# Five chunks of six of a normalized token block turned by VectorE squares and a trip through memory, and its columns kept in triples

## The chip, the cores and the metric

The kernel runs on one NeuronCore of one Trainium2 chip. The metric is the device time of one execution in microseconds (us). Three runs of the kernel before took 1774.83, 1776.05 and 1778.08 us; the median, 1776.05 us, is the time before.

## What is computed

The input `x` holds 8 images of 128 channels and 48 x 48 = 2304 positions (tokens), all in float32. Two layers follow each other; cut to what matters here:

```
# layer 0: causal attention over the tokens, queries and keys from a group-normed x and position rows
x = x + conv_attention(group_norm(x))            # softmax over the lower triangle, 128 channels
# layer 1, on tokens t = x seen as (image, token, channel)
xh = (t - mean(t)) / sqrt(var(t) + 1e-5)         # over the 128 channels of a token
t  = t + softmax(xh @ xh.T) @ xh                 # full self-attention of the 2304 tokens
t2 = layer_norm(t)
t  = t + scan(sigmoid, batch_norm(t2 @ W.T), V)  # a recurrence over the tokens
```

The change concerns `xh`. The product `xh @ xh.T` contracts over channels, so TensorE needs `xh` with the channels on the 128 partitions (channel-major). The product of the softmax with `xh` contracts over tokens, so it needs `xh` with the tokens on the partitions (token-major). The kernel holds both forms of an image.

## The kernel before, in words

An image is cut into 6 chunks of 384 tokens (`QC`), a chunk into 3 blocks of 128 (`QB`). `fast_path` walks over the images. For each one a `Causal` part goes through layer 0's attention and a `Full` part through layer 1's attention; the list `stream` (line 1414) is the order of all their items. One item is a score matmul (`begin`), an exponential on ScalarE, and three items later (`LAG`) the matmul with the values (`product`). A float32 matmul stands in the trace as two instructions.

After the last item of causal chunk j, `Causal.after` (line 1042) adds a chain of steps that makes chunk j of `xh`. For chunks 0 to 4 (`far`) it is: `store` (VectorE has turned the result in 32 x 32 squares at line 953; SyncE writes it to memory, line 961), `turn` (line 1062: VectorE transposes the softmax sums into the single-buffered tile `ta` and reduces them), `load` (line 967: four transfers bring the result back token-major), `sums` (TensorE adds the sums up, line 1072, and VectorE takes reciprocals), `residual` (line 1086, and the moments at lines 915 and 916), `rooted` (GpSimd, line 924), `normed` (line 929: VectorE writes the token-major chunk `c["y"]`, a part of `xhT`), and `back` (line 1103: three transposes on TensorE at line 934 into the PSUM tile `tb`, and one ScalarE copy at line 1105 into the channel-major tile `xh`). Chunk 5 takes the same steps, except that its result gets token-major by TensorE (`oc_t`) and not through memory.

The order of the work is written out by a planner, `Stream` (lines 548 to 601). It keeps a planned time `now` that TensorE work moves on (`spend`), and a planned time `at` from which a chain's next step may be put out. `tick`, after each item, puts out up to two steps that are due, in the order in which the chains were added. What it decides is only the order of the instructions in each engine's queue; at run time every queue is worked off in that order, and each instruction waits for its operands. `chunk_tile` (line 689) with a holder forces an earlier chain on to a given step before its tile is taken again.

`Full.begin` (line 1191) asks in chunk j = 0 that chunk n of `xh` has been put out before item 3n (line 1196), then issues the score matmul (line 1214), whose two operands are a block of 128 columns and a chunk of 384 columns of `xh`. The other half of the symmetric scores is not computed again: `turned` (line 1177) transposes the exponentials in squares, `store` (line 1157) writes them to memory as `e`, and `load` (line 1148) brings them back as `g`. All these transfers are issued by SyncE, whose queue is worked off in order; so are the position rows `pb` (line 845), the tokens `t1t` (line 1060), and `t_d` and `t2x` of the second normalization.

A recurrence of 36 steps for three segments follows at the end (line 1547).

Of the kernel before, what the change touches and what calls it, by code (L numbers as in the profile page):

```python
# [14 lines left out]
F32 = mybir.dt.float32  # L15
# [589 lines left out]
def fast_path(ctx: ExitStack, tc: tile.TileContext, x, pe, w_ffn, out, x_tok, w_qkv, w_pos, v_t, gamma_beta, flag):  # L605
    nc = tc.nc
    B, C, H, W = x.shape
    N = H * W
    P = 128
# [3 lines left out]
    QC = 384  # L613
    NQ = N // QC
    QB = QC // P
# [6 lines left out]
    dpool = ctx.enter_context(tc.tile_pool(name="dram", bufs=1, space=DRAM))  # L622
# [17 lines left out]
    SQ = 32  # L640
    R = P // SQ
# [22 lines left out]
    with ExitStack() as actx:  # L664
# [19 lines left out]
        def psum_t(name):  # L684
            return ps_t.tile([P, CH], F32, tag="t", name=name)
# [3 lines left out]
        def chunk_tile(tag, name, holder=None, steps=0, bufs=2):  # L689

            if holder is not None:
                before = holders.setdefault(tag, deque([({}, 0)] * bufs))
                old, n = before.popleft()
                before.append((holder, steps))
                if "chain" in old:
                    st.advance(old["chain"], n)
            return (work if bufs == 2 else work1).tile([P, QC], F32, tag=tag, name=name)
# [247 lines left out]
        def turn_result(o, name, holder, blocks_first):  # L945

            ot = chunk_tile("o", f"ot_{name}", holder, 1)
            dst, src = ot.rearrange("p (a g c) -> p a g c", a=R, g=QB), o[:, :QC]
            if blocks_first:
                dst, src = dst.rearrange("p a g c -> p g a c"), src.rearrange("p (g a r) -> p g a r", a=R, g=QB)  # L950
            else:
                src = src.rearrange("p (a g r) -> p a g r", a=R, g=QB)
            nc.vector.transpose(dst, src)
            return ot
# [16 lines left out]
        def block_of(to, g):  # L971

            return to.rearrange("p (k g c) -> p g k c", g=QB, c=SQ)[:, g]

        def by_block(tile_ap):

            return tile_ap.rearrange("p (g a r) -> p a g r", a=R, g=QB)
# [3 lines left out]

        t1_tok, x_hat, normed_chunks = {}, {}, {}

        class Causal:


# [55 lines left out]
            def after(self, j, o):  # L1042
                b = self.b
                cols = ts(j, QC)
                acc = self.sums.pop(j)[1]
                c = self.whose.pop(j)

                far = CAUSAL_FAR and j < NQ - 1
                if far:
                    ot = turn_result(o, f"c_{b}_{j}", c, False)  # L1050
                    at = st.then(st.now, [("DVE", 0.57)])
                    through = token_major(c, ot, f"c_{b}_{j}", "toc", 5)
                else:
                    o_sb = chunk_tile("o", f"oc_{b}_{j}", c, 3)
                    nc.scalar.copy(by_block(o_sb), o[:, :QC].rearrange("p (a g r) -> p a g r", a=R, g=QB))
                    at = st.then(st.now, [("ACT", 0.5)])
                    through = []

                y = t1p.tile([P, QC], F32, tag="t1t", name=f"t1t_{b}_{j}")
                nc.sync.dma_start(y, x_tok[b, j])  # L1060

                def turn():
                    ta = chunk_tile("ta", f"ta_{b}_{j}", bufs=1)
                    nc.vector.transpose(ta, acc)
                    c["parts"] = small.tile([P, R * QB], F32, tag="parts", name=f"parts_{b}_{j}")
                    nc.vector.tensor_reduce(c["parts"], ta.rearrange("p (k c) -> p k c", c=SQ), AX.X, ALU.add)

                def sums():

                    tp = psum_t(f"dn_{b}_{j}")  # L1070
                    k = R * QB
                    nc.tensor.matmul(tp[:, :k], same.rearrange("p a c -> p (a c)"), c["parts"], start=True, stop=True)  # L1072
                    own = small.tile([P, R, QB], F32, tag="ownc", name=f"ownc_{b}_{j}")
                    nc.vector.tensor_mul(own.rearrange("p a g -> p (a g)"), tp[:, :k], mine[:, 0].rearrange("p a g -> p (a g)"))
                    ri = small.tile([P, QB], F32, tag="ric", name=f"ric_{b}_{j}")
                    nc.vector.tensor_reduce(ri, own.rearrange("p a g -> p g a"), AX.X, ALU.add)
                    nc.vector.reciprocal(ri, ri)
                    c["ri"] = ri

                def residual():  # L1080
                    to = None if far else transposed(o_sb, f"oc_t_{b}_{j}")
                    for g in range(QB):
                        yg = y[:, ts(g, P)]
                        if far:
                            yg = yg.rearrange("p (k c) -> p k c", k=R)
                        nc.vector.scalar_tensor_tensor(
                            yg, block_of(c["o"], g) if far else to[:, ts(g, P)], c["ri"][:, g : g + 1], yg, ALU.mult, ALU.add
                        )
                    t1_tok[b, j] = y
                    c["mv"], c["ve"] = moments(y, f"c{b}_{j}", "l1")  # L1090

                def rooted():
                    c["rs"] = root(c["ve"], f"c{b}_{j}", "l1")

                def normed():
                    if j == 0:
                        x_hat[b] = (
                            big.tile([P, NB, P], F32, tag="xhT", name=f"xhT_{b}"), big.tile([P, N], F32, tag="xh", name=f"xh_{b}")
                        )
                    c["y"] = x_hat[b][0][:, QB * j : QB * (j + 1), :].rearrange("p g c -> p (g c)")  # L1100
                    normalize(c["y"], t1_tok[b, j], c["mv"], c["rs"])

                def back():
                    tp = transposed(c["y"], f"tb_{b}_{j}")
                    nc.scalar.copy(x_hat[b][1][:, cols], tp[:, :QC])

                c["chain"] = normed_chunks[b, j] = st.add([
                    *through[:1],
                    (turn, 0.0, [("DVE", 1.05)]),
                    *through[1:],  # L1110
                    (sums, 0.15, [("DVE", 0.55)]),
                    (residual, 0.0 if far else 0.35, [("DVE", 2.6)]),
                    (rooted, 0.0, [("POOL", 0.9)]),
                    (normed, 0.0, [("DVE", 1.1)]),
                    (back, 0.35, [("ACT", 0.5)]),
                ], max(at, st.free["DVE"]) + 0.2 - st.now)

        class Full:
# [72 lines left out]
            def begin(self, j, what, first):  # L1191
                b = self.b
                if first and j == 0:
                    self.rows = small2.tile([P, NB, NQ], F32, tag="rows", name=f"rows_{b}")
                if j == 0:
                    st.finish(normed_chunks[b, what[1] // QB])
                if first and b + 1 < B:
                    if j == 1:
                        norm_chain[b + 1] = st.add(group_norm(b + 1))
                    if j == NQ - 2:  # L1200
                        st.finish(norm_chain[b + 1])
                        project(b + 1, 0)
                self.prefetch()
                if what[0] == "turned":
                    i, g = what[1:]
                    while (i, j) not in self.loaded:
                        while self.pairs[len(self.loaded)] not in self.stored:
                            self.store()
                        self.load()
                    return self.loaded[i, j][:, :, g, :, :].rearrange("p a m r -> p m a r"), 0.0  # L1210
                m = what[1]
                xh = x_hat[b][1]
                s = psum_s(f"s1_{b}_{j}_{m}")
                nc.tensor.matmul(s[:, :QC], xh[:, ts(m, P)], xh[:, ts(j, QC)], start=True, stop=True)  # L1214
                p = pp.tile([P, QC], F32, tag="p", name=f"p1_{b}_{j}_{m}")
                nc.scalar.activation(p, s[:, :QC], AF.Exp, bias=shift, accum_out=self.rows[:, m, j : j + 1])  # L1216
                return p, st.then(st.spend(QC * US), [("ACT", 0.58)])
# [208 lines left out]
        for n in range(len(stream) + LAG):  # L1426
            if n < len(stream):
                part, j, what, first, last = stream[n]
                ready[n] = part.begin(j, what, first)
            if n >= LAG:  # L1430
                part, j, what, first, last = stream[n - LAG]
# [16 lines left out]
    with ExitStack() as rctx:  # L1448
# [32 lines left out]
        a = rc.tile([P, 1], F32, tag="bn_a", name="bn_a")  # L1481
        rsqrt(rc, a, mv[:, 1:2], 1e-5, "bn")
        nc.vector.tensor_mul(a, a, gb[:, 0:1])
        c = rc.tile([P, 1], F32, tag="bn_c", name="bn_c")
# [19 lines left out]
        prev, warm, y = [], [], [None] * G  # L1504
# [7 lines left out]
        d = rc.tile([P, G, B, SG], F32, tag="d", name="d")  # L1512
# [25 lines left out]
        for t in range(-WARM, LS):  # L1538
            s = t % TZ
# [93 lines left out]
```

## Time and profile before

| What | Value |
|---|---|
| Median of three runs | 1776.05 us |
| Span of the profiled execution (first to last instruction) | 1772.5 us |
| What lies around the span, against the median | 3.55 us |
| Mean granted TensorE clock | 0.993 |
| TensorE busy | 1742.7 us (98%) |
| VectorE busy | 1302.8 us (74%) |
| ScalarE busy | 764.8 us (43%) |
| GpSimd busy | 195.2 us (11%) |
| Transposes `tb`, line 934 | 144 of 273 ns, 23.6 us busy |
| Copies `xh<-tb`, line 1105 | 48 of 478 ns |
| Score matmuls `s<-xh`, line 1214 | 504 in 1008 instructions, 410.4 us busy |
| SyncE transfers | 257.47 MB |

The page gives no own time of the profiled execution apart from its span; the three runs were timed without the profiler. In the profile, PE is TensorE's matmuls, PEld its weight loads, DVE VectorE, ACT ScalarE, POOL GpSimd and SP SyncE; a q behind the name is the engine's queue, with its transfers and waits. A group of instructions is told by line, engine and operation, then what it writes and reads. Busy times of TensorE overlap where matmuls are pipelined; the chain of work that ended last gives each piece the time by which it moved the end. Images repeat: the main loop has a period of 207.7 us per image, and the views below look at the third image (about 463 to 671 us).

### The profile page before, as it was taken

What the parts mean: (1) busy time and instruction counts of PE and PEld (TensorE: products, weight loads), DVE (VectorE), ACT (ScalarE), POOL (GpSimd) and SP (SyncE); (2) the same over time, 40 slices, a digit from 0 to 9 for tenths busy, and PEclk for the clock granted to TensorE, in tenths of its full rate; (3) what the DMA queues carried; (4) which work ended last, traced back from release to release, by engine and by line L of the source; (5) the groups of instructions that cost most, each with busy time, mean ns of one, the idle gap of its engine ahead of it and who ended that gap; (6) DMA issues with size and microseconds to landing.
All of it is one profiled execution on the core that took longest, in us unless ns stands there. A gap on an engine that the chain in (4) does not pass through costs nothing.

```text
span 1772.5 us, 22223 instructions
## 1 busy us (share of the span) xinstructions
PE 1742.7 (98%) x6231; PEld 1093.2 (62%) x6231; DVE 1302.8 (74%) x3363; ACT 764.8 (43%) x1842; POOL 195.2 (11%) x303
## 2 busy tenths in 40 slices
PE   8999999999999999999999999999999999999996
PEld 5666566665666566665666656665666656665565
DVE  4868668876887668786687767876687866877467
ACT  2344434443345434444344433454344543444455
POOL 1110011100110001100111001100011001110006
PEclk8999999999999999999999999999999999999998
DMA  4405672257533584156732575335941468116768
GB/s 140 138 23 187 182 204 94 87 184 188 145 103 128 159 226 141 34 176 182 200 99 80 188 192 152 106 111 161 237 129 50 160 183 214 45 65 198 194 211 216
DMA packets 206056, 262.00 MB, mean 148 GB/s; under 512 B 90113, under 2 KB 175010, under 8 KB 205412
## 3 DMA queue, kind: packets, MB, share of 16 engines
q1 hardware_dynamic: 204972, 257.47, 49.4%
q0 software_dynamic: 720, 2.62, 1.0%
q8 instruction: 52, 0.85, 0.2%
q14 instruction: 80, 0.66, 0.1%
q10 hardware_dynamic: 232, 0.40, 0.1%
HBM read 150.24 MB, written 110.17 MB: 147 GB/s over the span
## 4 chain that ended last, share of the span: by engine, by line
PE 96%; DMA 1%; DVE 1%; ACT 0%; issue 0%; SPq 0%; POOL 0%; ACTq 0%; POOLq 0%; DVEq 0%
PE o L1228 18%; PE s L1214 18%; PE s L1013 17%; PE o L1024 17%; PE o L1224 13%; PE pj L874 4%; PE pj L877 2%; PE z L1547 2%; PE wx L1320 2%; PE of_t L934 1%; PE tb L934 1%; PE pb L832 0%; DMA x<-in_x_dram 0%; PE dn L1072 0%; PE ts L1259 0%
## 5 line engine op out<-in xcount | busy, mean ns | idle before, releaser
L1216 ACT ACTIVATE p<-s,shift 128x384 f32<-128x384 f32 x504 | 292.4, 580 | 479.7 <-PE s L1214 464.2
L1015 ACT ACTIVATE p<-s 128x384 f32<-128x384 f32 (+2 forms) x504 | 231.8, 460 | 424.8 <-PE s L1013 377.5
L1214 PE MATMUL s<-xh 128*128 128x384 f32 x1008 | 410.4, 489 | 0.0
L1228 PE MATMUL o<-p,xhT 128*128 128x384 f32 x1008 | 404.1, 488 | 5.9 <-ACT p L1216 5.9
L1013 PE MATMUL s<-q,k 128*128 128x384 f32 (+2 forms) x1008 | 381.5, 460 | 0.2 <-DVE k L884 0.2
L1024 PE MATMUL o<-p,vT 128*128 128x384 f32 (+2 forms) x1008 | 377.4, 456 | 0.0
L1224 PE MATMUL o<-g,xhT 128*128 128x384 f32 x720 | 281.3, 488 | 1.1 <-DMA g<-e 1.1
L1228 PEld LDWEIGHTS o<-p,xhT 128*128 128x128 f32 x1008 | 188.9, 190 | 133.8 <-ACT p L1216 10.5
L1024 PEld LDWEIGHTS o<-p,vT 128*128 128x128 f32 x1008 | 188.8, 190 | 114.7 <-issue 0.6
L1214 PEld LDWEIGHTS s<-xh 128*128 128x128 f32 x1008 | 186.2, 190 | 115.3
L1013 PEld LDWEIGHTS s<-q,k 128*128 128x128 f32 x1008 | 182.6, 191 | 97.3 <-issue 1.0
L1039 DVE TENSOR_TENSOR acc<-acc,p 128x384 f32<-128x384 f32 (+2 forms) x408 | 208.8, 512 | 33.4 <-POOL p L1018 8.7
L1177 DVE STREAM_TRANSPOSE t<-p 128x384 f32<-128x384 f32 x360 | 187.3, 550 | 37.6 <-ACT p L1216 32.8
L1224 PEld LDWEIGHTS o<-g,xhT 128*128 128x128 f32 x720 | 133.2, 190 | 83.7 <-DMA g<-e 1.3
L1185 DVE TENSOR_REDUCE tsum<-t 128x12 f32<-128x1152 f32 x120 | 162.3, 1353 | 4.2
L879 DVE TENSOR_TENSOR z<-pj,pb 128x384 f32<-128x384 f32 x144 | 78.8, 547 | 108.8 <-PE pj L874 92.4
L1018 POOL TENSOR_TENSOR p<-p,triu 128x128 f32<-128x128 f32 x144 | 72.5, 505 | 606.2 <-ACT p L1015 475.2
L1294 POOL TENSOR_TENSOR roots<-ve_f,mhalf 128x3 f32<-128x3 f32 x48 | 40.7, 849 | 521.8 <-DVE ve_f L918 521.8
L1216 ACT ACTIVATION_READ_ACCUMULATOR p<-s,shift 128x1 f32 x504 | 97.2, 193 | 0.0
L874 PE MATMUL pj<-xn,wT 128*128 128x384 f32 x192 | 79.7, 500 | 1.4 <-DVE xn L867 1.4
L924 POOL TENSOR_TENSOR rs_c<-ve_c,mhalf 128x3 f32<-128x3 f32 x48 | 45.1, 939 | 216.2 <-DVE ve_c L918 213.6
L1321 DVE TENSOR_TENSOR scale<-wx,scale 128x384 f32<-128x384 f32 x46 | 25.4, 551 | 56.1 <-PE wx L1320 50.3
(264 smaller groups left out, 1485.6 us busy)
## 6 DMA issues: line engine op xcount, KB each, us to landing
e<-t SPq DMA_DIRECT2D x120, 576.0 KB
g<-e SPq DMA_DIRECT2D x480, 144.0 KB
pb<-posb_d SPq DMA_DIRECT2D x46, 576.0 KB
t1t<-in_x_tok_dram SPq DMA_DIRECT2D x48, 192.0 KB
t_d<-tt SPq DMA_DIRECT2D x184, 48.0 KB
t2x<-t_d SPq DMA_DIRECT2D x46, 192.0 KB
scale<-rs SPq DMA_DIRECT2D x46, 192.0 KB
x<-in_x_dram SPq DMA_DIRECT2D x14, 576.0 KB
```

The costliest lines, as they stand in the source:

```text
L874: nc.tensor.matmul(ps[:, :QC], wT[:, j, :], xn, start=True, stop=True)
L879: nc.vector.tensor_add(z, ps[:, :QC], c["pb"][:, j, :])
L1013: nc.tensor.matmul(s[:, off:QC], keys[b][:, ts(m, P)], queries[b, j][:, off:], start=True, stop=True)
L1015: nc.scalar.activation(p[:, off:], s[:, off:QC], AF.Exp, scale=SCALE)
L1024: nc.tensor.matmul(o[:, off:QC], vals[b][:, ts(m, P)], p[:, off:], start=first, stop=last)
L1039: nc.vector.tensor_add(a[:, off:], a[:, off:], p[:, off:])
L1177: nc.vector.transpose(t[:, :, :, g, :].rearrange("p b j r -> p j b r"), p.rearrange("p (j b r) -> p j b r", j=QB, b=R))
L1185: nc.vector.tensor_reduce(self.tsum[j][:, n - j - 1, :], t.rearrange("p b j m r -> p (b j) (m r)"), AX.X, ALU.add)
L1214: nc.tensor.matmul(s[:, :QC], xh[:, ts(m, P)], xh[:, ts(j, QC)], start=True, stop=True)
L1216: nc.scalar.activation(p, s[:, :QC], AF.Exp, bias=shift, accum_out=self.rows[:, m, j : j + 1])
L1224: nc.tensor.matmul(out_ap, xhT[:, QB * i + g, :], p, start=first, stop=last)
L1228: nc.tensor.matmul(o[:, :QC], xhT[:, what[1], :], p, start=first, stop=last)
```

## The change

For chunks 0 to 4 of each image, `back` is replaced by three steps. `squares` transposes the normalized chunk on VectorE in 32 x 32 squares into a tile `ty`, which shares the single buffer of `ta`. `put` writes it to memory, as one transfer of 192 KB. `fetch` reads it back with four transfers of 32 partitions each, which set the squares in their places. Chunk 5 keeps `back`.

The columns of a chunk of `xh` are no longer stored block after block but in triples: column x of the three blocks stand side by side. So the runs that `fetch` reads are 96 elements (384 bytes) long, and the two operands of the score matmul at line 1214 step through `xh` by three elements (12 bytes). `turn` now takes its tile with an empty holder, so that the two uses of the buffer are put out in order.

```
+        def xh_chunk(b, j):
+            return x_hat[b][1][:, ts(j, QC)].rearrange("p (x g) -> p g x", g=QB)
+
+        def xh_block(b, m):
+            return xh_chunk(b, m // QB)[:, m % QB]
...
                 def turn():
-                    ta = chunk_tile("ta", f"ta_{b}_{j}", bufs=1)
+                    ta = chunk_tile("ta", f"ta_{b}_{j}", {}, bufs=1)
...
                 def back():
                     tp = transposed(c["y"], f"tb_{b}_{j}")
-                    nc.scalar.copy(x_hat[b][1][:, cols], tp[:, :QC])
+                    nc.scalar.copy(xh_chunk(b, j), tp[:, :QC].rearrange("p (g x) -> p g x", g=QB))
+
+                def squares():
+                    c["ty"] = chunk_tile("ta", f"ty_{b}_{j}", c, 8, bufs=1)
+                    nc.vector.transpose(
+                        c["ty"].rearrange("p (k c g) -> p g k c", k=R, g=QB), c["y"].rearrange("p (g k c) -> p g k c", g=QB, k=R)
+                    )
+
+                def put():
+                    c["xh_d"] = dpool.tile([P, QC], F32, tag="xh_d", name=f"xh_d_{b}_{j}")
+                    nc.sync.dma_start(c["xh_d"], c["ty"])
+
+                def fetch():
+                    d = c["xh_d"].rearrange("(a i) (k f) -> k i a f", a=R, k=R)
+                    for k in range(R):
+                        nc.sync.dma_start(x_hat[b][1][ts(k, SQ), cols].rearrange("i (a f) -> i a f", a=R), d[k])
+
+                if far:
+                    backs = [
+                        (squares, 0.0, [("DVE", 0.6)]),
+                        (put, 0.0, [("", 5.0)]),
+                        (fetch, 0.0, [("", 5.0)]),
+                    ]
+                else:
+                    backs = [(back, 0.35, [("ACT", 0.5)])]
...
                     (normed, 0.0, [("DVE", 1.1)]),
-                    (back, 0.35, [("ACT", 0.5)]),
+                    *backs,
...
                 m = what[1]
-                xh = x_hat[b][1]
                 s = psum_s(f"s1_{b}_{j}_{m}")
-                nc.tensor.matmul(s[:, :QC], xh[:, ts(m, P)], xh[:, ts(j, QC)], start=True, stop=True)
+                nc.tensor.matmul(s[:, :QC], xh_block(b, m), xh_chunk(b, j), start=True, stop=True)
```

## The prediction

> **What bounds the kernel now.** I read four views in this order: the page's busy shares with the chain of work that ended last, TensorE's own waits, the busy time of two stages of one image, and the instructions around the change in that image.
>
> ```profile
> PE 1742.7 (98%) x6231; PEld 1093.2 (62%) x6231; DVE 1302.8 (74%) x3363; ACT 764.8 (43%) x1842; POOL 195.2 (11%) x303
> ...
> PE 96%; DMA 1%; DVE 1%; ACT 0%; issue 0%; SPq 0%; POOL 0%; ACTq 0%; POOLq 0%; DVEq 0%
> PE o L1228 18%; PE s L1214 18%; PE s L1013 17%; PE o L1024 17%; PE o L1224 13%; PE pj L874 4%; PE pj L877 2%; PE z L1547 2%; PE wx L1320 2%; PE of_t L934 1%; PE tb L934 1%; PE pb L832 0%; DMA x<-in_x_dram 0%; PE dn L1072 0%; PE ts L1259 0%
> ```
>
> TensorE makes 96% of the chain, and the transposes that the change takes away (tb, line 934) stand in it. Whatever leaves TensorE's queue shortens the end by its own time, as long as TensorE never waits. Between 300 and 1600 us it waits once in all, 3.8 us for exponentials:
>
> ```profile
> PE o L1228 <- ACT p L1216: 3.8, 6, 0.6
> ```
>
> So no other engine sets the pace. The next view is the causal stage and the full stage of the third image, with each engine's busy time:
>
> ```profile
> 463.50:535.75 72.25, 72.25 (x267) 46.01 (x266) 58.89 (x169) 31.18 (x63) 10.93 (x18) 1.00 0.28 88
> 535.75:671.20 135.45, 134.82 (x467) 82.38 (x466) 97.14 (x242) 58.04 (x153) 9.17 (x13) 1.00 0.62 178
> ```
>
> In the causal stage VectorE, the third engine figure, is busy for 58.89 us of 72.25 (82%), and the transfers take 0.28 of the DMA engines. There is room for a little more of both.
>
> **What the Trainium skill says.** First, "SBUF — State Buffer", Specifications: a line of SBUF has 16 bytes, full bandwidth needs at least two hits in a line, and each step to a new line costs. Its section on Door 1 says that four fp32 elements can be strided for free. At 12 bytes, four elements touch three lines, so the two sentences disagree. The trace has a 96-byte case, which costs, and a 12-byte one, which does not; they come below. Second, "VectorE: DVE Perf Modes", The three transpose paths: VectorE turns 32 x 32 blocks only. The kernel's squares agree (570 ns for 128 x 384), and this is why the trip through memory is needed. Third, "DMA: Bandwidth & Descriptors", Two DMAs through the same engine are not ordered: the issuing engine must wait on the first one's semaphore. So SyncE's queue stands still between put and fetch, as it does today between lines 961 and 967.
>
> **The change part by part.**
>
> Removed from TensorE: three transposes for each of 5 x 8 = 40 chunks. Each takes 273 ns, but they overlap; in the chain of the third image three of them move the end by this much:
>
> ```profile
> 511.02 0.33 PE tb L934 x3
> ```
>
> The chain's finer answer gives tb 0.9% of 1772.5 us, 16.0 us for 48 triples, again 0.33. So 40 x 0.33 = **13.2 us** go, all of it on the path.
>
> Removed from ScalarE: 40 copies of 478 ns, 19.1 us. ScalarE is 43% busy and TensorE doesn't wait for it, so I count nothing.
>
> Added to VectorE: 40 squares. The nearest row is line 1288, the same transpose with runs of 32 in its output, 577 ns. Here the output steps by 12 bytes. Lower bound 0.57; upper bound 2.36 x 0.577 = 1.36 us, from ScalarE's worst stride below. I take 0.6: 3 us per image, 6.8 at most. They come where tb stood (493, 511, 523, 531 and 543 us), which is after the stretch from 470 to 490 us where VectorE is 92% busy. Cover: accumulations at line 1039 wait behind a square, but six `p` buffers and three items (3.9 us) stand between them and TensorE. Cost 0; without cover up to 0.6 us x 40 = 24 us.
>
> A new wait: `turn` and `ty` share one buffer, so a `turn` after a put waits for its landing, with the accumulations behind it. Of the third image's turns (480.8, 500.2, 506.5, 525.9, 540.3 us) only the one at 525.9 comes near a put (that of chunk 2, from 523.3 + 0.6 on). A transfer of this kind, line 961, is issued at 518.35 us; the wait for it lasts 1.4 us after its issue took 0.32, so it lands after about 1.75 us. The put then lands about 526.5: under 1 us of wait, 2 at most, hidden by VectorE's gap of 3.12 us before 534.6. Cost 0.
>
> SyncE: one put and four fetches, 5 x 0.43 = 2.2 us of issue, and 1.8 us standing still, about 4 us per chunk and 20 us per image. What is queued behind: `load` and `store` of the next chunk, `pb`, `t1t`, `t2x`, and at chunk 4 the first `e`. SyncE already waits up to 12.4 us at line 967 without hurting TensorE:
>
> ```profile
> SPq L967 <- DVE st_c L915: 202.5, 32, 12.4
> ```
>
> Traffic grows by 40 x 2 x 192 KB = 15.7 MB on 262 (6%), in the stage where 0.28 is in use. Cost 0.
>
> Where it could come late: chunk 4, the last to take the long way. Item 12 needs it:
>
> ```profile
> 540.86 0.55 DVE L1066 TENSOR_REDUCE parts<-ta 128x12 f32<-128x384 f32 x1
> 544.15 0.17 DVE L1074 TENSOR_TENSOR ownc<-dn,mine 128x12 f32<-128x12 f32 x1 [2.73 <-PE dn L1072]
> ```
> ```profile
> 524.93 0.43 SPq L1060 DMA_DIRECT2D t1t<-in_x_tok_dram  x1
> 549.11 6.67 SPq L1157 DMA_DIRECT2D e<-t  x3
> ```
> ```profile
> 543.49 0.49 PE L934 MATMUL tb<-ident,xhT 128*128 128x128 f32 x3
> ...
> 552.12 0.81 PE L1214 MATMUL s<-xh 128*128 128x384 f32 x2
> ```
>
> VectorE is free from 541.4 to 544.15, so the square runs at 541.4 to 542.0. SyncE's queue is empty from 525 to 549 us, so put is issued at 542.1 and lands at 543.9 to 545. The four fetches then take 1.74 us to issue (line 967's row) and 1.8 to land: 547.5 to 548.5. Item 12 starts at 552.12 - 0.33 = 551.8. Slack 3 us, cost 0. This holds if fetch stands in SyncE's queue ahead of the first `e` store, which waits until 549.11. By the planner, squares goes out about 543.5, put one tick later (544.9) and fetch 5.15 us after that, at the tick of 550.4. The `e` store is due about 549.3 to 550.0 (the third square of its tile, behind the 2.6 us of residual) and goes out when the next item begins, just after that tick. It is close, about one item.
>
> The operands in triples: line 1214's 504 matmuls (410.4 us busy, 18.5% of the chain, 328 us) read 12-byte steps. No TensorE row of before has such a step. What the trace has on strides is this: ScalarE reading 96-byte steps against contiguous, and VectorE reading 12-byte steps (line 1268) against contiguous elements (line 1264):
>
> ```profile
> L1341 ACT COPY t2c<-t2x 128x384 f32<-128x384 f32 x46 | 51.8, 1126 | 3.6 <-DMA t2x<-t_d 3.6
> ...
> L1105 ACT COPY xh<-tb 128x384 f32<-128x384 f32 x48 | 23.0, 478 | 14.6 <-PE tb L934 13.5
> ```
> ```profile
> L1268 DVE TENSOR_REDUCE more<-own 128x3 f32<-128x60 f32 x8 | 1.9, 232 | 0.3
> L1264 DVE TENSOR_TENSOR own<-ts,mine 128x60 f32<-128x60 f32 x8 | 1.8, 220 | 9.0 <-PE ts L1259 9.0
> ...
> L1268 DVE TENSOR_REDUCE more<-own 128x3 f32<-128x12 f32 x8 | 1.3, 166 | 0.3
> ...
> L1264 DVE TENSOR_TENSOR own<-ts,mine 128x12 f32<-128x12 f32 x8 | 1.3, 158 | 1.5 <-PE ts L1259 1.5
> ```
>
> From 12 to 60 elements line 1268 grows by 66 ns (1.4 ns an element) and line 1264 by 62 (1.3). At 12 bytes the stride costs VectorE nothing to speak of. TensorE takes a column of a float32 matmul every 0.84 ns (0.645 us / 2 / 384), about ScalarE's pace of one element in 0.84 ns (between its 128 and 384 wide exponentials, 277 and 490 ns). I take 0. No mechanism makes a strided read faster than a dense one, so the lower bound is 0. Upper bound: ScalarE's strided element costs (1126 - 478) / 384 + 0.84 = 2.5 ns; if that is the price of a line, three lines in four elements make 1.9 ns against 0.84, 2.25 times. The weight loads, 190 ns each, have 322 ns to hide in.
>
> Chunk 5's copy writes 12-byte steps: 8 times, at most 0.65 us more, about 0.5 us ahead of its use. Cost 0 to 2 us.
>
> **Sum.** 1772.5 - 13.2 = 1759.3 us of span; with the 3.55 us by which the median lies above this execution's span (0.2%), 1762.9. I say **1763.0 us**, 0.73% faster. Some 0.2% is what a measurement can tell from no change.
>
> **Rivals.**
>
> Slower, the triples: TensorE pays for the stride. For it: the skill's price for each new line and the ScalarE row. Against it: line 1268. Full price 328 x 1.25 = 410 us, 1763 + 410 = 2173 us. It decides from 4% on the strided matmul: 0.04 x 328 = 13.1 us eats the gain. Chance 0.11.
>
> The late fetch takes the place of the transposes: the `e` store gets ahead of fetch in SyncE's queue. Then fetch is issued from 549.5 to 551.3 us and lands about 553.1 to 553.8; TensorE stands 1.3 to 2 us at item 12 in each image, 10 to 16 us in all: 1773 to 1779, say **1776 us**, no change. With a landing as long as the 4.84 us that a `t2x` shows near the end it would be 1795. For it: one item of room. Against it: the order by planned times. Chance 0.15.
>
> Part given back: waits at `turn` and the crowded SyncE queue cost TensorE 0.5 to 1 us an image, 4 to 8 us: 1767 to 1771, say **1769 us**. Chance 0.08.
>
> The forecast, 1760 to 1767 us, has 0.66.
>
> **Range and chances.** From 1760 to 1779 us holds the forecast, the part given back and most of the late fetch, about 0.85; the stride case stays out. Faster by over 0.2% (under 1772.5): 0.66 + 0.08 + 0.02 = 0.76. Within 0.2% (to 1779.6): 0.09 of the late fetch. Slower: 0.11 + 0.04 = 0.15.
>
> **What would show it.** Right: 24 of the 144 tb transposes are left, line 1214 keeps 486 to 489 ns per instruction, TensorE's waits don't grow, and each image's period falls from 207.7 to about 206.0 us. Squares near 0.58 us. Wrong: longer instructions at the score matmul (the stride), or a TensorE wait of 1 us or more on the transfer into xh at item 12 with SyncE held at the `e` store before it (the late fetch), or ScalarE waiting for acc with a VectorE wait at `turn` in front of it.

## The result, and the profile after

| | Before | After |
|---|---|---|
| Median, same chip | 1775.44 us (4 runs) | 2012.29 us (4 runs) |
| Span of the profiled execution | 1772.5 us | 2009.3 us |
| Mean granted TensorE clock | 0.993 | 0.977 |

The change makes the kernel 13.4% slower: the ratio is 1.134, interval 1.132 to 1.135. The forecast was 1763.0. The span grew by 236.8 us, and this is what has to be explained. The busy shares and the chain of work that ended last, from the page of the kernel after:

```profile
PE 1931.1 (96%) x6111; PEld 1159.7 (58%) x6111; DVE 1331.0 (66%) x3403; ACT 748.5 (37%) x1802; POOL 202.7 (10%) x303
PE 91%; DVE 4%; DMA 3%; SPq 1%; issue 1%; ACT 0%; POOL 0%; ACTq 0%; POOLq 0%; DVEq 0%
PE s L1245 24%; PE o L1259 15%; PE s L1021 15%; PE o L1032 15%; PE o L1255 11%; PE pj L874 3%; PE pj L877 2%; PE z L1578 1%; PE wx L1351 1%; PE of_t L934 1%; DMA xh<-xh_d 1%; DVE t L1209 1%; DMA xh_d<-ty 1%; DVE xhT L929 1%; SPq L1128 0%
```

TensorE has 120 instructions fewer (the 40 triples of transposes) and is busy for 188 us more. The score matmul, line 1214 before and 1245 now, went from 18% to 24% of a longer chain. And the chain is no longer TensorE's alone: VectorE, transfers and SyncE's queue make 8% of it, where they made 2%, with the put and the fetch (`xh_d<-ty`, `xh<-xh_d`) among them. Of the signs that the prediction named as wrong, the first (longer score matmuls) is there, and of the second the wait at item 12, though no `e` store holds SyncE any more when TensorE waits. First the groups, the columns being busy time, mean ns of one, and idle time before it:

```profile
L1245 PE MATMUL s<-xh 128*128 128x384 f32 x1008 | 607.0, 688 | 54.4 <-DMA xh<-xh_d 54.4
L1117 DVE STREAM_TRANSPOSE ty<-xhT 128x384 f32<-128x384 f32 x40 | 27.6, 691 | 0.0
L1113 ACT COPY xh<-tb 128x384 f32<-128x384 f32 x8 | 5.5, 683 | 9.0 <-PE tb L934 9.0
```

The score matmul's instruction takes 688 ns, where 486 to 489 were expected. Then TensorE's waits:

```profile
PE s L1245 <- DMA xh<-xh_d: 54.4, 8, 7.9
```

Eight waits on the transfer into `xh`, one in each image: 0.5 us in the first and 7.6 to 7.9 us in each of the other seven. The third image's instructions at item 12, first TensorE's, then SyncE's, then VectorE's:

```profile
606.53 0.82 PE L1259 MATMUL o<-p,xhT 128*128 128x384 f32 x2
615.24 1.62 PE L1245 MATMUL s<-xh 128*128 128x384 f32 x2 [7.89 <-DMA xh<-xh_d]
```
```profile
603.48 0.34 SPq L1189 DMA_DIRECT2D e<-t  x1
609.79 0.34 SPq L1123 DMA_DIRECT2D xh_d<-ty  x1
611.66 1.74 SPq L1128 DMA_DIRECT2D xh<-xh_d  x4
613.45 0.43 SPq L1189 DMA_DIRECT2D e<-t  x1
```
```profile
594.84 0.87 DVE L1094 SCALAR_TENSOR_TENSOR t1t<-to_c,ric,t1t 128x128 f32<-128x128 f32 x3
...
606.47 0.82 DVE L929 TENSOR_SCALAR xhT<-t1t,mv_c,rs_c 128x128 f32<-128x128 f32 x3
607.82 1.35 DVE L1217 TENSOR_REDUCE tsum<-t 128x12 f32<-128x1152 f32 x1
609.09 0.67 DVE L1117 STREAM_TRANSPOSE ty<-xhT 128x384 f32<-128x384 f32 x1
```

The put is issued the moment the square ends, at 609.79, and the fetch 1.87 us later. No `e` store stands between them; one went out at 603.48, ahead of the put, and then SyncE had nothing to do but wait for the square. What is late is the square: it runs at 609.09, when item 12, due at about 607.3, has already been waiting. Chunk 4's residual (line 1094) ran at 594.84, some 12.5 us ahead of item 12. Before, it ran at 535.51 and item 12 at 552.12, 16.6 us.

The first image shows the same kernel with the square in time. Here it runs 8.3 us ahead of item 12's due time (139.2 us), and although an `e` store does stand between put and fetch, TensorE waits 0.5 us. Item 12, then VectorE's and SyncE's instructions:

```profile
139.66 1.34 PE L1245 MATMUL s<-xh 128*128 128x384 f32 x2 [0.47 <-DMA xh<-xh_d]
```
```profile
130.90 0.66 DVE L1117 STREAM_TRANSPOSE ty<-xhT 128x384 f32<-128x384 f32 x1
```
```profile
131.58 0.34 SPq L1123 DMA_DIRECT2D xh_d<-ty  x1
135.33 0.34 SPq L1189 DMA_DIRECT2D e<-t  x1
135.72 2.37 SPq L1128 DMA_DIRECT2D xh<-xh_d  x4
```

Last, the granted clock behind the third image's wait. The columns are the window, its length, busy time of the five engines, PEclk, DMA share and GB/s:

```profile
607.00:615.20 8.20, 0.34 (x2) 0.00 (x0) 5.40 (x9) 0.41 (x2) 0.00 (x0) 0.66 0.28 89
615.20:618.00 2.80, 2.76 (x5) 1.47 (x6) 0.40 (x1) 0.67 (x2) 0.00 (x0) 0.50 0.96 239
618.00:620.50 2.50, 2.50 (x8) 1.72 (x7) 0.18 (x1) 1.09 (x2) 0.00 (x0) 0.61 0.96 358
620.50:625.00 4.50, 4.50 (x12) 2.38 (x11) 3.08 (x5) 1.61 (x6) 0.00 (x0) 1.00 0.71 205
```

After the wait TensorE runs at half its clock for nearly 5 us: 2.80 x 0.50 + 2.50 x 0.39 = 2.4 us of work are lost. That agrees with the Trainium skill, "TensorE: Matmul & The Clock Gate", Part 1: The HAM clock gate: after an idle stretch the clock falls to half.

From this comes a first theory with two parts. **The stride** of 12 bytes slows the matmul itself. **The late square**, a matter of the order written by the planner and not of any engine's speed, makes the wait and the half clock. The rivals to the first: it is the weight's stride and not the moving operand's, or the larger SyncE and DMA traffic. The rivals to the second: SyncE's queue, or the two trips through memory being too slow in themselves.

### The profile page after: what moved, and what is told of

It reads as the page before. It is cut to its first block, busy times and chain, and to the rows that moved or that the text cites. A ratio compares the mean times of both kernels' runs of the same rounds, so it can differ in the third digit from the quotient of the medians.

```text
span 2009.3 us, 22270 instructions
## 1 busy us (share of the span) xinstructions
PE 1931.1 (96%) x6111; PEld 1159.7 (58%) x6111; DVE 1331.0 (66%) x3403; ACT 748.5 (37%) x1802; POOL 202.7 (10%) x303
## 4 chain that ended last, share of the span: by engine, by line
PE 91%; DVE 4%; DMA 3%; SPq 1%; issue 1%; ACT 0%; POOL 0%; ACTq 0%; POOLq 0%; DVEq 0%
PE s L1245 24%; PE o L1259 15%; PE s L1021 15%; PE o L1032 15%; PE o L1255 11%; PE pj L874 3%; PE pj L877 2%; PE z L1578 1%; PE wx L1351 1%; PE of_t L934 1%; DMA xh<-xh_d 1%; DVE t L1209 1%; DMA xh_d<-ty 1%; DVE xhT L929 1%; SPq L1128 0%
## 5 line engine op out<-in xcount | busy, mean ns | idle before, releaser
L1245 PE MATMUL s<-xh 128*128 128x384 f32 x1008 | 607.0, 688 | 54.4 <-DMA xh<-xh_d 54.4
L1259 PE MATMUL o<-p,xhT 128*128 128x384 f32 x1008 | 411.9, 496 | 0.4 <-ACT p L1247 0.4
L1259 PEld LDWEIGHTS o<-p,xhT 128*128 128x128 f32 x1008 | 199.2, 199 | 238.1 <-issue 170.1
L1245 PEld LDWEIGHTS s<-xh 128*128 128x128 f32 x1008 | 247.2, 254 | 141.7 <-issue 50.7
```

What stands on the lines that cost most here:

```text
L1245: nc.tensor.matmul(s[:, :QC], xh_block(b, m), xh_chunk(b, j), start=True, stop=True)
L1259: nc.tensor.matmul(o[:, :QC], xhT[:, what[1], :], p, start=first, stop=last)
```

## The experiments

Each kernel is compared with the kernel before in runs on the same chip (medians 1773.5 to 1774.6 us); its span is set against 1772.5. Five of the kernels (both operands in triples, dense moving operand with the long way, and the moving operand in steps of 8, 12 and 16 bytes) have one run each; the runs of the kernel before lie between 1771.5 and 1778.4 us, and the smallest effect read from a single run is 12.6 us.

**One operand at a time.** On the kernel before, first the moving operand alone in 12-byte steps, then the weights alone.

```
+ mv = xh[:, ts(j, QC)].rearrange("p (x g) -> p g x", g=3)
+ nc.tensor.matmul(s[:, :QC], xh[:, ts(m, P)], mv, start=True, stop=True)
```

> The kernel before with one edit: the 384 columns of the score matmul's moving operand are read with 12-byte steps; its weights stay dense, and there are no squares and no trip through memory. The columns of the scores come in another order, so what is computed is permuted. Theory, the moving stride: the instruction moves the end by about 0.505 us instead of 0.322 as in the changed kernel, so 1008 x 0.183 = 184 us more, about 1960 us. Rival, the strided weights: nothing is lost here, about 1775 us. Rival, the late fetch: about 1775 us too.

```
+ wt = xh[:, ts(m // QB, QC)].rearrange("p (x g) -> p g x", g=QB)[:, m % QB]
+ nc.tensor.matmul(s[:, :QC], wt, xh[:, ts(j, QC)], start=True, stop=True)
```

> The kernel before with one edit: the 128 columns of the score matmul's weights are read with 12-byte steps; its moving operand stays dense. The rows of the scores come in another order, so what is computed is permuted. Theory, the moving stride: the weight load takes 252 ns instead of 190 as in the changed kernel, but stays hidden behind 322 ns of matmul, 1775 to 1779 us. Rival, the strided weights: about 1960 us, with the matmul records at some 680 ns.

Measured: 1951.05 us with the moving operand strided (span +176.6), 1778.49 with the weights strided (ratio 1.0022, interval 1.0014 to 1.0029). The matmul and weight load groups of the two kernels, in this order:

```profile
L1215 PE MATMUL s<-xh 128*128 128x384 f32 x1008 | 595.0, 675 | 0.0
L1215 PEld LDWEIGHTS s<-xh 128*128 128x128 f32 x1008 | 186.2, 190 | 115.2
```
```profile
L1215 PE MATMUL s<-xh 128*128 128x384 f32 x1008 | 414.5, 493 | 0.0
L1215 PEld LDWEIGHTS s<-xh 128*128 128x128 f32 x1008 | 248.0, 252 | 88.7
```

The stride of the moving operand alone costs 176.6 us, with the old schedule and nothing sent through memory. The weight load also gets longer, 190 to 252 ns, but most of that lies under the matmul before it: it costs 4 to 6 us. There is no sign of the traffic in this.

**The triples without the long way.** On the kernel after, every chunk goes back to TensorE and the columns stay in triples.

```
- if far:
+ if far and False:
```

> The changed kernel with all six chunks turned back on TensorE: columns in triples and both operands strided, but no squares, no put and no fetch. Theory, the stride makes most of the loss: about 1775 + 190 = 1965 us, and no TensorE wait on a transfer into xh. Rival, the trip through memory makes most of it: about 1780 us.

Measured: 1957.11 us, span 1955.2, so +182.7. No TensorE wait on `xh` from memory is left. Its groups:

```profile
L1245 PE MATMUL s<-xh 128*128 128x384 f32 x1008 | 599.8, 680 | 0.0
L1113 ACT COPY xh<-tb 128x384 f32<-128x384 f32 x48 | 32.6, 678 | 14.6 <-PE tb L934 13.5
```

The layout alone is worth 182.7 of the 236.8 us: 176.6 for the moving operand, and another 6, about what the weights cost by themselves. ScalarE's copy pays for the stride as well, 478 to 678 ns in 48 copies, and nobody waits for it.

**The other strides.** The prediction had to guess how the price depends on the step. Two more steps of the moving operand, with `mv` as in the first kernel above; only its grouping differs, g=2 in one kernel and g=4 in the other:

```
- mv = xh[:, ts(j, QC)].rearrange("p (x g) -> p g x", g=3)
+ mv = xh[:, ts(j, QC)].rearrange("p (x g) -> p g x", g=2)
```

> As e1, but the moving operand is read with 8-byte steps, two elements to each 16-byte line (the scores' columns come in another order, so what is computed is permuted). Theory, a line costs as much as two elements and no more: nothing is lost, 1775 to 1790 us. Rival, the price grows with the number of lines: e1's 0.175 us for half a line an element more makes 0.088 us for a quarter, 1775 + 88 = about 1863 us.

> As e1, but the moving operand is read with 16-byte steps, one element to each line (what is computed is permuted). Theory, a line costs as much as two elements: each instruction moves the end by 0.65 to 0.67 us instead of 0.322, 1775 + 1008 x 0.34 = about 2115 us. Rival, the price grows evenly with the lines: 0.175 x 1.5 = 0.263 us more, about 2040 us.

Measured: 1786.92 us (span +12.6) at 8 bytes and 2120.89 us (span +346.4) at 16. The groups of the two kernels:

```profile
L1215 PE MATMUL s<-xh 128*128 128x384 f32 x1008 | 425.7, 503 | 0.0
```
```profile
L1215 PE MATMUL s<-xh 128*128 128x384 f32 x1008 | 762.7, 846 | 0.0
```

One dense instruction moves the end by 0.3225 us (0.645 for the two of a matmul). Adding each kernel's growth of the span, shared among 1008 instructions, and dividing by 384 columns:

| Step of the moving operand | us per instruction | ns per column | against dense |
|---|---|---|---|
| 4 bytes | 0.3225 | 0.84 | 1 |
| 8 bytes | 0.335 | 0.87 | 1.04 |
| 12 bytes | 0.498 | 1.30 | 1.54 |
| 16 bytes | 0.666 | 1.73 | 2.07 |

At 16 bytes each column has a line of 16 bytes for itself, and costs 1.73 ns. At 8 bytes two columns share a line, 0.87 each: 1.74 for the line. At 12 bytes four columns touch three lines, and 3 x 1.73 / 4 = 1.30. So a line costs about 1.73 ns, the time of two dense columns, and one law gives all three strides; wider steps were not run. It is the law that the prediction tried for its upper bound, with 1.73 in place of its 2.5 ns. The Trainium skill, "SBUF — State Buffer", says both things: Specifications, that full bandwidth needs two hits in a line, which these runs bear out to 4%; and Door 1, that four fp32 elements can be strided for free, which they contradict. On TensorE that step doubles the time.

**The late square by itself.** On the kernel after, the moving operand is read densely again. The scores' columns then come in triples, and the exponential reads them from PSUM with 12-byte steps, which puts them in order.

```
- nc.tensor.matmul(s[:, :QC], xh_block(b, m), xh_chunk(b, j), start=True, stop=True)
+ nc.tensor.matmul(s[:, :QC], xh_block(b, m), x_hat[b][1][:, ts(j, QC)], start=True, stop=True)
...
+ pg = p.rearrange("p (g x) -> p g x", g=QB)
+ sg = s[:, :QC].rearrange("p (x g) -> p g x", g=QB)
+ nc.scalar.activation(pg, sg, AF.Exp, bias=shift, accum_out=self.rows[:, m, j : j + 1])
```

> The changed kernel with one edit: the moving operand is read densely, in the order in which the triples lie, and ScalarE's exponential puts the columns in order as it reads PSUM. Squares, put, fetch and the strided weights are kept, and so is the order that the planner writes. Theory, the moving stride and the late fetch together: the stride's 184 us go and the waits of about 54 us stay, 1776 - 13 + 54 = 1817 us. If the waits are only a consequence of the slowed matmuls: about 1763 us. Rival, the strided weights or the path itself: near 2000 us. ScalarE's exponential stays at 580 ns if PSUM's strided read is free.

Measured: 1849.87 us, span +75.6, more than expected. Its group of the score matmul, and four windows of its third image:

```profile
L1245 PE MATMUL s<-xh 128*128 128x384 f32 x1008 | 427.7, 507 | 65.8 <-DMA xh<-xh_d 65.8
```
```profile
566.00:573.00 7.00, 0.41 (x1) 0.44 (x2) 4.00 (x6) 0.00 (x0) 0.00 (x0) 0.63 0.36 116
573.00:574.50 1.50, 1.50 (x3) 0.74 (x3) 0.00 (x0) 0.25 (x1) 0.00 (x0) 0.50 0.95 263
576.00:578.00 2.00, 2.00 (x5) 1.09 (x5) 0.00 (x0) 1.22 (x3) 0.00 (x0) 0.50 1.04 394
578.00:580.00 2.00, 2.00 (x8) 1.40 (x7) 0.75 (x2) 0.79 (x4) 0.00 (x0) 0.98 1.05 231
```

The stride's cost is gone and the wait has grown to 9.1 or 9.2 us in seven images (1.8 us in the first), probably because the twelve items ahead of it pass faster. From about 572.6 to 578 us TensorE works at half its clock, 2.7 us lost; over all images it is 21 us. The sum: -13.2 (transposes) + 65.8 (waits) + 21 (clock) + 4 (weights) = 78 us against 75.6 measured. My expectation had left the half clock out. In the chain of work of this image the put takes 1.86 us and the fetch's landing 1.80, as the prediction had them, so the trips are not slow in themselves.

**The order, two ways.** On that kernel, first chunk 4 as well goes back to TensorE, so that no chunk on the long way is near its use.

```
- if far:
+ if far and j < NQ - 2:
```

> The kernel of e4 (moving operand dense, columns put in order by the exponential's read of PSUM) with one more edit: chunk 4 too is turned back on TensorE, so that only chunks 0 to 3 take squares, put and fetch. Theory, only chunk 4 comes too late: TensorE's waits on the transfer into xh go, with the half clock after them. 32 triples of 0.33 us are saved (10.6 us), the strided weights cost what e2 showed (0.2%, 3.9 us): 1774.6 - 10.6 + 3.9 = about 1768 us. Rival, the trip through memory also costs by its share of VectorE and of SyncE's queue: 1775 us or more, with waits of TensorE for exponentials or of other kinds.

Second, only planned times are changed. No instruction is added, removed or altered; what changes is where each stands in its queue.

```
- return [(store, 0.0, [("", 5.0)]), (load, 0.0, [("", 5.0)])]
+ return [(store, 0.0, [("", 2.0)]), (load, 0.0, [("", 4.0)])]
...
- (put, 0.0, [("", 5.0)]),
- (fetch, 0.0, [("", 5.0)]),
+ (put, 0.0, [("", 2.0)]),
+ (fetch, 0.0, [("", 4.0)]),
```

> The kernel of e4 with other planned prices: store and put are planned with 2 us instead of 5, load and fetch with 4 instead of 5; nothing else is changed. So only the order of the instructions moves: the square of chunk 4 is put out some 5 items ahead of item 12, not with it. Theory, the order holds chunk 4 up: the wait at item 12 falls from 8.2 us to 0 to 4 us an image, and the half clock after it goes with a wait below about 3 us: 1770 to 1805 us. Rival, the transfers themselves are slow (put and fetch 5 us and more, or a full SyncE queue): the wait stays at 7 us or more and the time near 1850 us.

Measured: 1776.0 us (ratio 1.0011, interval 1.0004 to 1.0018) and 1776.26 us (1.0015, 1.0007 to 1.0024). TensorE's waits of the first, then of the second:

```profile
PE s L1245 <- ACT xh L1113: 6.1, 8, 0.8
PE o L1257 <- DMA g<-e: 3.3, 6, 0.8
```
```profile
PE s L1245 <- ACT xh L1113: 5.3, 7, 0.8
PE o L1257 <- DMA g<-e: 4.0, 6, 1.2
```

In the second the same five chunks take the same way through the same queue, and the wait of 65.8 us is gone with the half clock: 74 us for a change of order alone. That the stall came from the order is thereby shown; slow transfers or a full SyncE queue would have stayed. Its third image: the square now runs at 543.46 us and the fetch is issued at 546.08.

```profile
543.46 0.68 DVE L1117 STREAM_TRANSPOSE ty<-xhT 128x384 f32<-128x384 f32 x1
```
```profile
544.17 0.34 SPq L1123 DMA_DIRECT2D xh_d<-ty  x1
546.08 1.78 SPq L1128 DMA_DIRECT2D xh<-xh_d  x4
```

Why the square was late stands in the planner's own times. These are the planned us at which the steps are put out in the second image; in the third each column repeats with an offset of its own:

```
                      before    after    short prices
chunk 4 turn          320.63   325.78    317.83
chunk 5 turn          335.21   337.45    332.06
chunk 4 residual      330.09   338.73    330.78
chunk 5 residual      339.55   342.72    338.61
chunk 4 normed        335.21   344.35    335.90
chunk 4 squares                350.43    337.33
chunk 4 put                    350.43    340.24
chunk 4 fetch                  350.43    342.80
item 12               346.30   350.43    342.80
```

Before, chunk 4's residual is put out 5.1 us ahead of chunk 5's turn; after, it comes 1.3 us behind it, and chunk 5's residual gets in ahead of chunk 4's normed. When normed is put out, at 344.35, the planner already has VectorE booked until 348.31, and so it plans the squares for 349.56, the put for 354.62 and the fetch for 359.77. The squares go out at 350.43, and item 12, which is begun then, forces out the other two with them. With the short prices, chunk 4's normed stays ahead of chunk 5's residual, and the squares go out 5.5 us ahead of item 12. Chains are served in the order in which they were added, with two steps per tick; that the two more steps in each chain and their planned VectorE time are what pushed chunk 4 back is read from these rules, and was not tried by itself. Nor was it tried which of the shorter prices sets it right.

The first kernel misses its 1768 us; the second lies in its range, but gains nothing either. The transposes taken away are worth 10.6 us (32 triples) and 13.2 us (40), so 12.4 and 14.9 us are lost by the spans of 1774.3 and 1774.2. The weights take 4 to 6. TensorE's waits on chunk 5's copy, on `g` and on exponentials come to 10.9 and 13.2 us, against 7.0 us of waits on `g` and exponentials in the kernel before, which makes 3.9 and 6.2. The rest, some 2.5 to 5 us, stays open.

**Dense columns through memory.** If the strides cost and the order is free, the columns should be stored block after block. Then the fetch has twelve transfers with runs of 32 elements instead of four with 96, again with the short prices.

```
- d = c["xh_d"].rearrange("(a i) (k f) -> k i a f", a=R, k=R)
+ d = c["xh_d"].rearrange("(a i) (k g c) -> k g i a c", a=R, k=R, g=QB)
...
+ for g in range(QB):
+     xh = x_hat[b][1][ts(k, SQ), ts(QB * j + g, P)]
+     nc.sync.dma_start(xh.rearrange("i (a c) -> i a c", a=R), d[k, g])
```

> The five chunks take squares, put and fetch, but a chunk's columns stay block after block, so that both operands of the score matmul, chunk 5's copy and the square's output are dense as before; fetch needs 12 transfers of 128-byte runs instead of 4 of 384-byte runs. Planned prices 2 us for store and put, 4 for load, 6 for fetch. Theory, what e6 lost was the strided weights (about 4 to 6 us) and the strided copy of chunk 5: 1773.5 - 13.2 + waits of 0 to 5 us = 1761 to 1767 us. Rival, five trips through memory cost what they save whatever the operands are: 1773 us or more, and 8 more issues per chunk (8 x 0.43 us on SyncE) make the waits on g and xh longer.

The same with chunk 4 back on TensorE:

```
- if far:
+ if far and j < NQ - 2:
```

> As e9, with chunk 4 turned back on TensorE too, so four chunks of six take the way through memory. Theory: 32 triples saved, 1773.5 - 10.6 + 0 to 4 us = 1763 to 1767 us, and no TensorE wait on a transfer into xh. Rival as in e9: 1773 us or more.

Measured: 1802.86 us with five chunks (ratio 1.0162, interval 1.0149 to 1.0176), and 1772.7 us with four (0.9989, 0.9983 to 0.9996): two misses. Of the first, TensorE's wait and SyncE's queue; of the second, TensorE's waits:

```profile
PE s L1247 <- DMA xh<-xh_d: 19.6, 7, 3.1
```
```profile
551.12 5.57 SPq L1130 DMA_DIRECT2D xh<-xh_d  x12
```
```profile
PE o L1257 <- DMA g<-e: 5.5, 7, 1.2
PE s L1247 <- ACT xh L1113: 4.0, 7, 0.6
```

Twelve transfers take SyncE 5.57 us to issue, against 1.78 for four, and for chunk 4 that reaches item 12: TensorE waits 2.6 to 3.1 us there in seven images, and behind five of these waits the clock is at half again (0.50 from 767.97 to 771.38 us, for one), so the mean granted clock is 0.987. With four chunks this wait is gone and the matmul keeps its pace (491 ns). It is the best version found and 0.1% faster than before, 1.4 us by the medians, where 32 triples are worth 10.6. Two stretches of its trace, from the first score matmul of one image's full stage to that of the next:

```profile
117.90:323.90 206.00, 205.53 (x718) 127.13 (x717) 156.51 (x405) 86.89 (x211) 21.73 (x31) 1.00 0.54 154
323.90:531.50 207.60, 206.11 (x720) 127.50 (x719) 156.98 (x412) 87.31 (x211) 20.79 (x31) 1.00 0.54 154
```

Before, such a stretch takes 207.67 us. The first is shorter by 1.67: twelve transposes (1.32 us) are gone, two instructions of `dn` fall outside it, and TensorE waits only 0.5 us. The second is as long as before, and so are those that follow (207.6 to 208.2 us). The gain is made once and then given back image by image: in the second stretch TensorE waits 0.6 us for `g`, 0.6 for chunk 5's copy and 0.3 for an exponential, where it waited 0.6 us in all before. That accounts for 0.9 of the 1.3 us; the rest is not explained.

## Why the prediction was wrong

- **Transposes, -13.2 us: right as far as it can be seen.** They left the chain, and 24 of 144 are left. Only the first stretch of the four-chunk kernel shows the gain nearly undisturbed (1.3 of its 1.67 us). That kernel had 10.6 us to win over the whole run, and its span is shorter by 2.9.
- **"I take 0" for the operands in triples: this step failed, by 182.7 us.** The mechanism was named as the slower rival, with the chance 0.11 and 410 us. The price of a line was too high there (2.5 ns against 1.73), so the matmul was to grow by 125% where it grew by 54%. What misled was the comparison of line 1268 with line 1264, 1.4 against 1.3 ns for an element. Line 1264 is no yardstick for a reduction: it is a product of two inputs, one of them in PSUM. The dense reductions of the kernel before, in its groups, give another pace:

```profile
L1185 DVE TENSOR_REDUCE tsum<-t 128x12 f32<-128x1152 f32 x120 | 162.3, 1353 | 4.2
L1066 DVE TENSOR_REDUCE parts<-ta 128x12 f32<-128x384 f32 x48 | 26.5, 553 | 1.6
```

  From 384 to 1152 elements they grow by 800 ns, 1.04 each. Against that, line 1268's 66 / 48 = 1.375 ns is slow by 1.32, and 1.375 x 4 / 3 = 1.83 ns for a line. By this yardstick, which rests on a few short reductions, the row that I read as free was paying the price, and it is near TensorE's 1.73. Applied to TensorE's 0.84 ns it would have given 1.375 / 0.84 = 1.64, some 209 us.
- **"Slack 3 us, cost 0" for chunk 4: this step failed, by 54.4 us of waits and the clock behind them.** Its condition, fetch ahead of the first `e` store in SyncE's queue, was not met, but that is not what cost the time: in seven images the first `e` store went out some 6 us ahead of the put (603.48 and 609.79 in the third), while the square was still to come. The failed part is "VectorE is free from 541.4 to 544.15, so the square runs" then: it took VectorE's gap of before as the square's place, and the planner's times of chunk 4 as they were. The order is computed again from all the steps, and in the new one chunk 5's steps come in between chunk 4's. The rival of the late fetch had the place right (item 12). Its mechanism, an `e` store between put and fetch, is there in the first image alone, where the wait is 0.5 us; in the other seven the mechanism is another, and the size is 7.6 to 7.9 us, not 1.3 to 2.
- **The half clock was in no case.** It follows the seven long waits, and half of TensorE's busy time at the clock of 0.50 makes 2.1 to 2.8 us for each, 17.0 us in all. The sum, 182.7 + 54.4 - 13.2 + 17.0 = 240.9 us, is 4 us above the 236.8 measured; that stays open.
- **Squares, 0.6 us:** 0.69, so the stride of 12 bytes in the output costs 120 ns; harmless, as was the wait at `turn`. **Chunk 5's copy, up to 0.65 us more:** 0.2 measured, 683 against 478 ns. It was to cost 0 to 2 us; in the kernels without the late square TensorE waits 4.0 to 6.1 us for it, also where the copy writes densely (4.0), so its place in the new order counts for more than its length.
- **The image's period**, forecast to fall to 206.0 us, rose. The windows of the third image in the kernel after, cut at line 874's first matmul and at the first score matmul of the full stage:

```profile
507.52:586.32 78.80, 78.80 (x284) 50.05 (x283) 68.48 (x184) 33.72 (x67) 13.25 (x20) 1.00 0.39 116
586.32:747.17 160.85, 152.11 (x435) 86.79 (x434) 91.28 (x230) 53.43 (x144) 7.83 (x11) 0.97 0.51 145
```

The two sum to 239.65 us, 32.0 more than the 207.67 of before between the same two instructions. The parts: 63 score matmuls by 1.01 - 0.645 us = 23.0, the wait 7.9, the clock 2.4, the transposes -1.65; together 31.6. From first score matmul to first score matmul, the step from the first image to the second, with its short wait, grows by 22.1 us, and the later ones by 30.7 to 32.0.

## What to carry to other kernels

Before an operand of the busiest engine is laid out anew, count the 16-byte lines that its access touches, and measure the pace of one strided instruction against a truly dense one of the same kind; a yardstick of another kind can hide the whole price. Where a planner writes the order, a step added to a chain can move the places of other chains' steps too, so the gaps of the old trace don't tell where new work will run: print the planner's new order before the slack is counted. A transpose taken off the bound engine is worth only its share of the chain (0.33 us a triple), and in these kernels new waits of half a microsecond used most of that up. Look at one period of the trace after another: here the first image differed from all others, in the changed kernel and in the best version.

## What was not expected of the hardware

- Strided writes to SBUF cost time too: ScalarE's copy with 12-byte steps takes 683 ns against 478, VectorE's square 691 against 569 (the four-chunk kernel with dense columns).
- A strided read of PSUM by ScalarE cost nothing: its exponential over 384 columns takes 580 ns in the dense moving kernel, where it reads PSUM with 12-byte steps, and 580 in the kernel before, where it reads densely.
- One wait of 8 us costs about 2.5 us more after it has ended, since the clock stays at half for some 5 us of work. Shorter waits can do it as well: in the kernel with five chunks and dense columns, five of seven waits of 2.6 to 3.1 us are followed by 3.4 us or more at a clock of 0.50.
